# A seven-product MLP's way down: sums and weight differences moved to VectorE, results taken out of PSUM before the residual is added

## The chip, the cores and the metric

The kernel runs on one core of a Trainium2 chip. Its time is the device time of the whole program in microseconds (us). Before the change it is 2821.14 us, the median of three runs (2816.69 to 2826.64). One more execution was recorded by the hardware profiler; every row below is from it.

Engines are named as in the profile: PE multiplies matrices (PEld is its weight load), DVE is VectorE, ACT is ScalarE, POOL is GpSimd, and SP issues the DMAs. PSUM is the memory into which PE writes its products; SBUF is the working memory.

## What is computed

Two transformer blocks with cross attention follow one another, on 16 sequences of 256 tokens with 512 channels. The case is about the MLP at the end of the first block:

```python
x = x + out
h = layer_norm(x, n2_w, n2_b)
h = jax.nn.gelu(h @ fc1_w + fc1_b, approximate=False) @ fc2_w + fc2_b
return x + h
```

fc1_w is 512 x 2048 and fc2_w is 2048 x 512. The second block takes the result. It also needs a mask that tells which of its rows are zero throughout: `mask0 = 1.0 - jnp.all(x == 0, axis=2, keepdims=True)`.

## The kernel before

**Three phases.** The first block's attention comes first, then its MLP (class `Mlp0`), then the second block with two attentions and an MLP. The 4096 rows are worked on in eight groups g of 512 rows (G = 4 tiles of 128 rows).

**Seven products.** The MLP's matrix products are done two by two blocks at a time, in the manner of Strassen and Winograd: seven block products in place of eight, for which some operands are first combined with one another. For the activations there are four such combinations ("sums", made by `differences`, lines 786 to 793 of the profile), for the weights four as well (`weigh`, lines 839 to 842). Afterwards the seven results are combined into the four blocks of the output.

**Two parts for precision.** Every operand is held as a high part and a low part: ACT casts the value to the high part (line 141, `x_t` in the profile, or `w_h`), and an engine subtracts that from the value to have the low part (line 142, `c_t` or `w_l`). Each block product is then three matmuls per piece: high by high, high by low, low by high.

**Way up (`up`).** fc1 and GELU; the hidden rows of each group and quarter are stored to HBM (`hid`), 1 MB each.

**Way down (`down`, from line 1167).** 32 steps n: for each group g four quarters q of the hidden rows. A step multiplies seven operands with fc2's weights, 84 matmuls of 256 columns, in the order of products 1, 6, 2, 7, 5, 4, 3. The seven results of a group stay in seven PSUM banks over its four steps; each of them has a pool tag (`mm`, `sc`, `pt`) with as many banks as there are results of that tag, so the next group takes a bank again when the result in it has been read. While step n runs, the operands of step n + 1 are made: `sums_down(n + 1)` makes the four sums, and after each product `write` makes the high and the low part of the operand that the product has just released. There is one copy of the operands, so an operand is rewritten between its product in step n and the same product in step n + 1.

In `differences` the first, third and fourth sum are made by `pool = nc.gpsimd` and the second by `own`, which is `nc.vector` here.

**The end of a group (`end`, line 1036).** In the step with q = 3 the results are combined after each product. ACT copies the result of product 1 out of PSUM (line 1046), DVE adds the others to it or straight into the residual rows `x` out of PSUM (lines 1048 to 1063), and POOL adds the two partial results that are in SBUF into `x` (lines 1049, 1050, 1055, 1056). Then the four tiles of `x` are stored (line 1065), ACT sums their absolute values (line 1068, `junk`) and DVE turns these into the mask (line 1071).

**The residual rows.** `residual(g)` (line 1027) loads four tiles of 128 x 512 into the one buffer with tag `x1`, in the step q = 1 (q = 2 for the first group); `offset` (line 1032) adds fc2's bias to them on POOL in the step q = 3. The load can start when the rows of the group before have been stored out of that buffer.

**Order.** PE's instructions run in the order in which the program has them. For the other engines a scheduler decides the order from a simulated timeline when the kernel is built, so an instruction may stand earlier or later in its queue than the program text suggests. On each engine they then run in that fixed order. All DMAs are issued by SP.

**Weights.** `weigh(way, m)` makes the combinations of weight block m: way 1 is fc1, way 2 fc2. The first two blocks of fc1 are made early, during attention; the other six at the start of the way up, the eight of fc2 during the last group of the way up and the first two steps of the way down.

Of the kernel before, what the change touches and what calls it, by code (L numbers as in the profile page):

```python
# [10 lines left out]
F32 = mybir.dt.float32  # L11
# [3 lines left out]
AF = mybir.ActivationFunctionType  # L15
ALU = mybir.AluOpType
# [4 lines left out]
P = 128  # L21
# [7 lines left out]
G = NB * NT  # L29
N = G * P  # L30
NG = B // NB
# [10 lines left out]
def kernel(ctx: ExitStack, tc: tile.TileContext, a, out):  # L42
# [7 lines left out]
    nc = tc.nc  # L50
# [22 lines left out]
    for t, at in ((0, 0), (1, P)):  # L73
        w = (t + 1) * P
        nc.gpsimd.affine_select(
            out=tri[:, at : at + w],
            in_=tri[:, at : at + w],
# [9 lines left out]
    for i in range(NB):  # L87
        own = hmask[:, i, i * HPC : (i + 1) * HPC]
        nc.gpsimd.memset(own, 1.0)
        for base, step in ((0, 1), (D - 1, -1)):  # L90
            nc.gpsimd.affine_select(
                out=own,
                in_=own,
# [8 lines left out]
    xd = [[dram.tile([N, C], F32, name=f"xd{i}_{g}") for g in range(NG)] for i in range(4)]  # L102
# [645 lines left out]
    class Mlp0:  # L748
# [13 lines left out]
        W = 2 * P  # L762
# [20 lines left out]
                self.open_group(m)  # L783


        def differences(self, a21, a22, a11, a12, out, own):

            s1, s2, s3, s4 = out
            pool = nc.gpsimd
            pool.tensor_tensor(out=s1, in0=a21, in1=a22, op=ALU.add)  # L790
            own.tensor_tensor(out=s2, in0=s1, in1=a11, op=ALU.subtract)  # L791
            pool.tensor_tensor(out=s3, in0=a11, in1=a21, op=ALU.subtract)
            pool.tensor_tensor(out=s4, in0=a12, in1=s2, op=ALU.subtract)
# [19 lines left out]
        def weigh(self, way, m, early=False):  # L813


            view = self.raw.pop(m)
            if way == 1:
                b = [[view[:, 2 * k : 2 * k + 2, ts(n, P)] for n in range(2)] for k in range(2)]
                b2 = view[:, 2:4, :].rearrange("p k (n c) -> p n k c", n=2)
            else:  # L820
                b = [[view[:, k, ts(n, 2 * P)] for n in range(2)] for k in range(2)]
                b2 = view[:, 1, :].rearrange("p (n c) -> p n c", n=2)
            self.w[m] = tuple(
                self.wp[m][1].tile([P, 7, 2 * P], F32R, tag=f"w{x}", name=f"w{m}_{x}")
                for x in "hl"
            )
            pool = self.tmp if not early and m % 2 and (way == 1 or m == 1) else self.pool
            diff = pool.tile([P, 4, 2 * P], F32, tag="diff", name="diff")

            def like(x):  # L830
                if way == 2:
                    return x
                if len(x.shape) == 2:
                    return x.rearrange("p (k c) -> p k c", k=2)
                return x.rearrange("p n (k c) -> p n k c", k=2)

            t1, t2, t3, t4 = (like(diff[:, i, :]) for i in range(4))
            pool = nc.gpsimd
            pool.tensor_tensor(out=t1, in0=b[0][1], in1=b[0][0], op=ALU.subtract)
            pool.tensor_tensor(out=t2, in0=b[1][1], in1=t1, op=ALU.subtract)  # L840
            pool.tensor_tensor(out=t3, in0=b[1][1], in1=b[0][1], op=ALU.subtract)
            pool.tensor_tensor(out=t4, in0=b[1][0], in1=t2, op=ALU.subtract)
            h, l = self.w[m]
            for x, at in ((b[0][0], 0), (b2, slice(1, 3))):
                split_lazy(x, like(h[:, at]), like(l[:, at]), nc.gpsimd if early else nc.vector)
            split_lazy(diff, h[:, 3:], l[:, 3:], nc.gpsimd if early else nc.vector)
# [137 lines left out]
        def sums_down(self, n):  # L984
            h = self.h.pop(n)
            b = [[h[:, :, k, ts(t, self.W)] for k in range(2)] for t in range(2)]
            if n == 0:

                s = [self.up_pool.tile([P, C], F32, tag="xn", name="sums") for _ in range(2)]
                two = self.tmp.tile([P, 4, 2 * P], F32, tag="diff", name="sums")  # L990
                two = two.rearrange("p (i m) n -> p i m n", m=2)
                s = [x.rearrange("p (m n) -> p m n", m=2) for x in s] + [two[:, i] for i in range(2)]
            else:
                s = self.px.tile([P, 4, 2, self.W], F32, tag="x2", name="sums")
                s = [s[:, i] for i in range(4)]
            self.differences(b[1][0], b[1][1], b[0][0], b[0][1], s, nc.vector)
            self.a = [b[0][0], b[0][1], b[1][1]] + s

        TAGS = {1: "mm", 6: "mm", 2: "mm", 7: "sc", 5: "sc", 4: "pt", 3: "pt"}
# [33 lines left out]
                    out=x[:, t, :], in0=x[:, t, :], in1=self.b_fc2, op=ALU.add  # L1033
                )

        def end(self, g, i, x):

            add, W = nc.vector.tensor_tensor, self.W
            p = self.banks

            def block(t, c):
                return x[:, 2 * t : 2 * t + 2, ts(c, W)]

            if i == 6:
                p1 = self.flat("p1")
                nc.scalar.copy(p1, p[g, 1])
                u2 = self.u2 = self.flat("u2")
                add(u2, p1, p[g, 6], ALU.add)
                nc.gpsimd.tensor_tensor(out=block(0, 0), in0=block(0, 0), in1=p1, op=ALU.add)
                nc.gpsimd.tensor_tensor(out=block(0, 1), in0=block(0, 1), in1=u2, op=ALU.add)  # L1050
            elif i == 2:
                add(block(0, 0), block(0, 0), p[g, 2], ALU.add)
            elif i == 7:
                add(self.u2, self.u2, p[g, 7], ALU.add)
                nc.gpsimd.tensor_tensor(out=block(1, 1), in0=block(1, 1), in1=self.u2, op=ALU.add)
                nc.gpsimd.tensor_tensor(out=block(1, 0), in0=block(1, 0), in1=self.u2, op=ALU.add)
            elif i == 5:
                add(block(0, 1), block(0, 1), p[g, 5], ALU.add)
                add(block(1, 1), block(1, 1), p[g, 5], ALU.add)
            elif i == 4:  # L1060
                add(block(1, 0), block(1, 0), p[g, 4], ALU.add)
            elif i == 3:
                add(block(0, 1), block(0, 1), p[g, 3], ALU.add)
                for t in range(G):
                    nc.sync.dma_start(out=xd[1][g][ts(t, P), :], in_=x[:, t, :])
                for t in range(G):
                    junk = self.flat("junk").rearrange("p m n -> p (m n)")
                    nc.scalar.activation(
                        junk, x[:, t, :], AF.Abs, accum_out=m0[:, g, t : t + 1]
                    )  # L1070
                nc.vector.tensor_scalar(m0[:, g, :], m0[:, g, :], 0.0, None, ALU.not_equal)

        def begin(self):

# [92 lines left out]
        def down(self, early, after_up):  # L1167
            last = NG * self.NS - 1
            left, load = ExitStack(), None
            xs = {}  # L1170
            self.hidden(1)
            for n in range(last + 1):
                g, q = divmod(n, self.NS)
                if n == last - 1:

                    for m in (2, 3):
                        self.wp[m][0].close()
                    load = early()
                    pool = sbuf(left, "late2", 1)
                    load(lambda: pool.tile([P, C], F32, tag="wst", name="wst", bufs=2))  # L1180

                    late = [pool.tile([P, N], F32R, name=f"late{i}") for i in range(6)]
                    late += [self.slots[7][1]]
                if q == (1 if g else 2):
                    xs[g] = self.residual(g)
                elif q == 3:
                    self.offset(xs[g])
                if n + 1 <= last:
                    self.sums_down(n + 1)
                    self.next = self.slots  # L1190
                    if n + 1 == last:
                        self.next = [(x, s[1]) for x, s in zip(late, self.slots)]
                if n + 2 <= last:
                    self.hidden(n + 2)
                for i in (1, 6, 2, 7, 5, 4, 3):
                    if n or i not in (1, 6):
                        self.product_down(n, i)
                    if n < last:
                        self.write(self.OPS[i][0])
                    if q == self.NS - 1:  # L1200
                        self.end(g, i, xs[g])
                    if n == last and i in (1, 2, 5, 4, 3):
                        after_up((1, 2, 5, 4, 3).index(i))
                self.at = self.next
                if n < 2:
                    self.weigh(2, self.NM - 2 + n)
            left.close()
            for m in range(4, self.NM):
                self.wp[m][0].close()
            self.tmp_stack.close()  # L1210
            for m in (1, 0):
                self.wp[m][0].close()
            self.stack.close()
# [380 lines left out]
```

## Time and profile before

| what | before |
|---|---|
| median of three runs | 2821.14 us |
| the profiled execution, its time | 2812.6 us |
| its span, first to last instruction | 2810.9 us |
| PE busy, share of the span | 95% |
| DVE | 73% |
| ACT | 65% |
| POOL | 31% |
| mean granted TensorE clock | 0.986 |
| way down: first to last matmul | 1071.2 to 1457.3 us |

The shares are means over three phases that differ. Rows of groups have: line, engine, operation, output <- inputs, shapes and count, then busy us and mean ns, then the idle time of the engine just before them and what ended it. Rows of waits have: the waiting engine, tile and line, what it waited for, then us in total, times, and the longest. Rows of a chain have: start, us, and what ran. A line number belongs to the kernel before; the helper lines 141 and 142 serve all of the MLP's operands.

### The profile page before, as it was taken

How to read it: one execution, taken by the hardware profiler on the slowest of the kernel's cores; microseconds unless marked ns; L12 is line 12 of the kernel's file. 1: busy time of each engine (PE TensorE's matmuls, PEld its weight loads, DVE VectorE, ACT ScalarE, POOL GpSimd, SP SyncE). 2: the span in 40 equal slices, each digit the busy share in tenths (PEclk: the TensorE clock that was granted, in tenths of full speed). 3: DMA queues.
4: the chain of work that ended last, by engine and by line, in shares of the span. 5: the costliest groups of instructions: out<-in, count | busy, mean ns of one | idle time of the engine just before them, and what ended most of it. 6: DMA issues, size and time to landing. Idle time of an engine off the chain costs nothing.

```text
span 2810.9 us, 56659 instructions
## 1 busy us (share of the span) xinstructions
PE 2676.1 (95%) x18970; PEld 2259.4 (80%) x18970; DVE 2045.4 (73%) x5763; ACT 1823.0 (65%) x5292; POOL 862.1 (31%) x874
## 2 busy tenths in 40 slices
PE   6999999998899999999989999999999999999998
PEld 5777777776799999889887787777777777777787
DVE  7666666657756559888876777777777777777887
ACT  4877777778555555343446787787777777777532
POOL 6222211204601127666661111113322122213333
PEclk9999999999999999999999999999999999999999
DMA  6565555644323334434356665657665555556221
GB/s 230 169 193 175 174 176 171 195 158 143 127 110 135 121 144 171 150 121 150 121 190 213 196 189 182 192 183 222 205 199 172 187 185 186 188 166 183 97 93 58
DMA packets 287810, 465.41 MB, mean 166 GB/s; under 512 B 36257, under 2 KB 188321, under 8 KB 279329
## 3 DMA queue, kind: packets, MB, share of 16 engines
q1 hardware_dynamic: 287520, 461.78, 51.0%
q8 instruction: 153, 2.51, 0.4%
q14 instruction: 137, 1.11, 0.1%
HBM read 284.97 MB, written 176.69 MB: 164 GB/s over the span
## 4 chain that ended last, share of the span: by engine, by line
PE 67%; DVE 15%; DMA 7%; issue 4%; ACT 3%; POOL 3%; SPq 1%; POOLq 0%; DVEq 0%; ACTq 0%
PE ps_p L258 17%; PE ps_v L258 14%; PE ps_pt L449 8%; PE down L1015 5%; PE ps_s L408 5%; PE ps_z L468 5%; PE up_sc L902 3%; DVE c_t L142 3%; PE up_pt L902 2%; PE up_mm L902 2%; PE ps_t L277 2%; DVE st L238 1%; DMA xd<-x 1%; ACT e L433 1%; DVE e L423 1%
## 5 line engine op out<-in xcount | busy, mean ns | idle before, releaser
L433 ACT ACTIVATE e<-e,mn 128x256 f32<-128x256 f32 (+1 forms) x1024 | 487.4, 480 | 66.3 <-DVE mn L423 63.9
L455 ACT COPY pt<-ps_pt 128x512 f32<-128x512 f32 (+1 forms) x696 | 378.2, 546 | 177.5 <-PE ps_pt L449 165.5
L449 PE MATMUL ps_pt<-ident,e 128*128 128x128 f32 x2816 | 437.0, 274 | 21.8 <-DVE lbias L1255 10.0
L449 PEld LDWEIGHTS ps_pt<-ident,e 128*128 128x128 f32 x2816 | 336.3, 141 | 62.9 <-ACT pt L455 7.6
L408 PE MATMUL ps_s<-stack 97*128 97x256 f32 (+1 forms) x1536 | 331.9, 298 | 15.0 <-ACT e L433 7.1
L408 PEld LDWEIGHTS ps_s<-stack 97*128 97x128 f32 (+1 forms) x1536 | 269.5, 190 | 74.5 <-ACT e L433 14.3
L1322 POOL TENSOR_TENSOR x<-x,zz 128x256 f32<-128x256 f32 x128 | 95.5, 746 | 727.9 <-DVE zz L1315 670.2
L1015 PE MATMUL down<-w_h,c_t 128*128 128x256 f32 x900 | 264.5, 295 | 21.5 <-DVE c_t L142 21.5
L433 ACT ACTIVATE e<-ps_s,mn 128x256 f32<-128x256 f32 x512 | 241.0, 483 | 53.9 <-DVE mn L419 43.9
L1015 PE MATMUL down<-w_h,x_t 128*128 128x256 f32 x868 | 254.8, 293 | 11.0 <-ACT x_t L141 8.8
L1015 PE MATMUL down<-w_l,x_t 128*128 128x256 f32 x868 | 253.3, 292 | 0.0
L423 DVE CUSTOM_DVE_ANT_0 e<-mb,ps_s 128x256 f32<-128x256 bf16 x512 | 192.6, 415 | 76.8 <-PE ps_s L408 74.8
L242 POOL TENSOR_TENSOR rstd<-rstd,nhalf 128x1 f32<-128x1 f32 x192 | 140.6, 738 | 316.6 <-DVE rstd L241 314.4
L258 PE MATMUL ps_p<-x_t,q_h 128*128 128x512 f32 x640 | 215.2, 417 | 4.4 <-DVE qk L128 2.3
L419 DVE TENSOR_REDUCE mn<-ps_s 128x2 f32<-128x512 f32 x256 | 175.0, 684 | 48.9 <-PE ps_s L408 46.6
L468 PE MATMUL ps_z<-pt,v 128*32 128x256 f32 (+1 forms) x3072 | 200.1, 369 | 4.3 <-ACT pt L455 2.1
L1015 PEld LDWEIGHTS down<-w_h,c_t 128*128 128x128 f32 x900 | 180.8, 201 | 25.0 <-DVE c_t L142 25.0
L423 DVE CUSTOM_DVE_ANT_0 e<-tri,ps_s 128x128 f32<-128x128 f32 (+1 forms) x512 | 160.1, 346 | 53.5 <-PE ps_s L408 51.4
L433 ACT ACTIVATION_READ_ACCUMULATOR e<-e,mn 128x1 f32 x1024 | 197.4, 193 | 0.0
L1015 PEld LDWEIGHTS down<-w_h,x_t 128*128 128x128 f32 x868 | 175.2, 202 | 12.5 <-ACT x_t L141 10.0
L141 ACT CAST x_t<-sums 128x512 fp32r<-128x512 f32 x156 | 92.6, 619 | 138.0 <-DVE sums L791 89.6
L1015 PEld LDWEIGHTS down<-w_l,x_t 128*128 128x128 f32 x868 | 175.0, 202 | 0.0
(245 smaller groups left out, 7463.6 us busy)
## 6 DMA issues: line engine op xcount, KB each, us to landing
stack<-d SPq DMA_DIRECT2D x1152, 128.0 KB
d<-qk SPq DMA_DIRECT2D x192, 512.0 KB
hid<-ho SPq DMA_DIRECT2D x32, 1024.0 KB
raw<-hid SPq DMA_DIRECT2D x32, 1024.0 KB
x<-xd SPq DMA_DIRECT2D x128, 256.0 KB
xd<-x SPq DMA_DIRECT2D x96, 256.0 KB
xin<-in_x_dram SPq DMA_DIRECT2D x32, 256.0 KB
xin<-in_ctx_dram SPq DMA_DIRECT2D x32, 256.0 KB
```

The costliest lines, as they stand in the source:

```text
L242: nc.gpsimd.tensor_tensor(out=rstd[:, 1:2], in0=rstd[:, 0:1], in1=nhalf, op=ALU.pow)
L258: nc.tensor.matmul(ps, w[p], x[q], start=(k == 0 and i == 0), stop=(k == kc - 1 and i == 2))
L408: nc.tensor.matmul(ps[:, t, :], u.st[: self.rows, 0, j, ts(t, P)], u.st[: self.rows, 1, j, :], start=True, stop=True,)
L419: nc.vector.tensor_reduce(mn, ps, AX.X, ALU.min)
L423: nc.vector.tensor_tensor_reduce(out=e[:, at], in0=bias[t], in1=ps[:, t, : job.width[t]], scale=-SC, scalar=BIG, op0=ALU.add, op1=ALU.min, ...
L433: nc.scalar.activation(e[:, at], ps[:, t, :] if bias is None else e[:, at], AF.Exp, bias=mn[:, t : t + 1], scale=-1.0, accum_out=u.rs[:, t ...
L449: nc.tensor.transpose(pp[:, ts(x, P)], e[:, at : at + P], ident)
L455: nc.scalar.copy(pt[:, :n], pp[:, :n])
L468: nc.tensor.matmul(z[ts(j, D), w[0] * P :], job.v[u.i * NT + mc][:, u.c * P + j * D : u.c * P + (j + 1) * D], u.pt[j][:, x0 * P : (x0 + le ...
L902: nc.tensor.matmul(ps[:, mm, :], w[p][:, k, :], x[q][:, k, :], start=(first and mm == k == j == 0), stop=(k == 1 and j == 2), skip_group_c ...
L1015: nc.tensor.matmul(ps[:, t, :], x[p][:, mm, ts(t, P)], w[r][:, bo, :], start=(q == mm == t == j == 0), stop=(q == self.NS - 1 and mm == 1 ...
L1322: nc.gpsimd.tensor_tensor(out=xv, in0=xv, in1=zz, op=ALU.add)
```

## The change

Four things are changed; the matmuls and their order are the same.

1. `differences` has a parameter for the engine of three of its sums. `sums_down` passes `nc.vector`, so all four sums of the way down are made on DVE. The way up's sums stay on POOL.
2. `weigh` uses DVE for its four differences where the weight block isn't one of the first two of fc1 (`early`).
3. `end` no longer touches the residual rows. It combines the results into four SBUF tiles: `p1`, `u2`, `u3` (pool tag `u`, three buffers) and `c22`.
4. A new `finish` adds these four to the residual rows, on DVE, then stores the rows and has ACT sum the absolute values. It stands in the program after product 2 of the next group's first step; `tests` (the mask) and the load of the next residual rows stand at q = 2 of the next group.

```diff
-        def differences(self, a21, a22, a11, a12, out, own):
+        def differences(self, a21, a22, a11, a12, out, own, pool=nc.gpsimd):
...
-            pool = nc.gpsimd
+            pool = nc.gpsimd if early else nc.vector
             pool.tensor_tensor(out=t1, in0=b[0][1], in1=b[0][0], op=ALU.subtract)
...
-            self.differences(b[1][0], b[1][1], b[0][0], b[0][1], s, nc.vector)
+            self.differences(b[1][0], b[1][1], b[0][0], b[0][1], s, nc.vector, nc.vector)
...
-        def end(self, g, i, x):
+        def end(self, g, i):
+            add, p = nc.vector.tensor_tensor, self.banks
             if i == 6:
-                p1 = self.flat("p1")
+                p1, u2 = self.flat("p1"), self.flat("u2")
                 nc.scalar.copy(p1, p[g, 1])
-                u2 = self.u2 = self.flat("u2")
                 add(u2, p1, p[g, 6], ALU.add)
-                nc.gpsimd.tensor_tensor(out=block(0, 0), in0=block(0, 0), in1=p1, op=ALU.add)
-                nc.gpsimd.tensor_tensor(out=block(0, 1), in0=block(0, 1), in1=u2, op=ALU.add)
+                self.c = [p1, u2]
             elif i == 2:
-                add(block(0, 0), block(0, 0), p[g, 2], ALU.add)
+                add(self.c[0], self.c[0], p[g, 2], ALU.add)
             elif i == 7:
-                add(self.u2, self.u2, p[g, 7], ALU.add)
-                nc.gpsimd.tensor_tensor(out=block(1, 1), in0=block(1, 1), in1=self.u2, op=ALU.add)
-                nc.gpsimd.tensor_tensor(out=block(1, 0), in0=block(1, 0), in1=self.u2, op=ALU.add)
+                u3 = self.flat("u3")
+                add(u3, self.c[1], p[g, 7], ALU.add)
+                self.c.append(u3)
             elif i == 5:
-                add(block(0, 1), block(0, 1), p[g, 5], ALU.add)
-                add(block(1, 1), block(1, 1), p[g, 5], ALU.add)
+                c22 = self.tmp.tile([P, 4, 2 * P], F32, tag="diff", name="c22")[:, :2, :]
+                add(self.c[1], self.c[1], p[g, 5], ALU.add)
+                add(c22, self.c[2], p[g, 5], ALU.add)
+                self.c.append(c22)
...
+        def finish(self, g, x):
+            for k, c in enumerate(self.c):
+                at = x[:, 2 * (k // 2) : 2 * (k // 2) + 2, ts(k % 2, self.W)]
+                nc.vector.tensor_tensor(at, at, c, ALU.add)
+                if k % 2:
+                    for t in (k - 1, k):
+                        nc.sync.dma_start(out=xd[1][g][ts(t, P), :], in_=x[:, t, :])
+            for t in range(G):
+                junk = self.flat("junk").rearrange("p m n -> p (m n)")
+                nc.scalar.activation(junk, x[:, t, :], AF.Abs, accum_out=m0[:, g, t : t + 1])
+
+        def tests(self, g):
+            nc.vector.tensor_scalar(m0[:, g, :], m0[:, g, :], 0.0, None, ALU.not_equal)
...
-                if q == (1 if g else 2):
+                if q == 2:
                     xs[g] = self.residual(g)
+                    if g:
+                        self.tests(g - 1)
...
-                        self.end(g, i, xs[g])
+                        self.end(g, i)
+                    if q == 0 and g and i == 2:
+                        self.finish(g - 1, xs.pop(g - 1))
...
+            self.finish(NG - 1, xs.pop(NG - 1))
+            self.tests(NG - 1)
```

More of the change, by code (lines that the diff above doesn't have):

```diff
@@ L837, in weigh @@
             t1, t2, t3, t4 = (like(diff[:, i, :]) for i in range(4))
-            pool = nc.gpsimd
+            pool = nc.gpsimd if early else nc.vector
             pool.tensor_tensor(out=t1, in0=b[0][1], in1=b[0][0], op=ALU.subtract)
@@ L1034, in offset @@
                 )
-        def end(self, g, i, x):
[L1038 to L1042, printed above, removed]
+        def end(self, g, i):
+            add, p = nc.vector.tensor_tensor, self.banks
             if i == 6:
-                p1 = self.flat("p1")
+                p1, u2 = self.flat("p1"), self.flat("u2")
                 nc.scalar.copy(p1, p[g, 1])
-                u2 = self.u2 = self.flat("u2")
@@ L1060, in end @@
+                add(self.c[1], self.c[1], p[g, 5], ALU.add)
+                add(c22, self.c[2], p[g, 5], ALU.add)
+                self.c.append(c22)
             elif i == 4:
-                add(block(1, 0), block(1, 0), p[g, 4], ALU.add)
+                add(self.c[2], self.c[2], p[g, 4], ALU.add)
             elif i == 3:
-                add(block(0, 1), block(0, 1), p[g, 3], ALU.add)
-                for t in range(G):
-                    nc.sync.dma_start(out=xd[1][g][ts(t, P), :], in_=x[:, t, :])
@@ L1066, in end @@
[L1066 to L1071, printed above, removed]
+                add(self.c[1], self.c[1], p[g, 3], ALU.add)
+        def finish(self, g, x):
[8 more added lines that the diff above has]
+                nc.scalar.activation(junk, x[:, t, :], AF.Abs, accum_out=m0[:, g, t : t + 1])
```

## The prediction

> **What bounds the kernel now.** I read the page first for the engine shares: PE is busy 95% of the span, so what can be won is where PE has gaps. The table by stretches finds them. The seven-product way down of the first MLP (its matmuls run from 1071.2 to 1457.3 us) has PE gaps; the way up before it is nearly dense. Columns: stretch, its length, then busy time and instruction count of PE, PEld, DVE, ACT and POOL, then clock, DMA share and GB/s. Each stretch is about one batch group of the way down (four steps):
>
> ```profile
> 1164.00:1211.00 47.00, 44.60 (x357) 44.19 (x357) 39.32 (x43) 20.50 (x40) 30.65 (x21) 0.96 0.40 136
> 1211.00:1258.00 47.00, 42.56 (x332) 41.95 (x332) 38.47 (x40) 18.26 (x37) 29.84 (x21) 0.93 0.40 135
> ```
>
> DVE (VectorE) 38 of 47 us and POOL (GpSimd) 30 of 47: neither full, both waiting on one another. The waits of 1071 to 1458 us say so:
>
> ```profile
> ACT x_t L141 <- DVE sums L791: 89.6, 27, 7.7
> ...
> POOL sums L790 <- DVE c_t L142: 59.7, 23, 4.2
> DVE sums L791 <- POOL sums L790: 49.0, 16, 6.5
> ...
> PEld down L1015 <- DVE c_t L142: 25.0, 17, 2.5
> ```
>
> The operand sums of a step go POOL, DVE, POOL; then ACT casts and DVE makes the low part (c_t), and PE waits for that. The groups of the same stretch give the durations:
>
> ```profile
> L142 DVE TENSOR_TENSOR c_t<-sums,x_t 128x512 fp32r<-128x512 f32 x123 | 132.5, 1102 | 5.9 <-ACT x_t L141 5.7
> ...
> L793 POOL TENSOR_TENSOR sums<-raw,sums 128x512 f32<-128x512 f32 x31 | 51.1, 1649 | 10.0 <-DVE sums L791 5.6 <-DVE m L1071 4.4
> L791 DVE TENSOR_TENSOR sums<-sums,raw 128x512 f32<-128x512 f32 x31 | 49.6, 1600 | 49.0 <-POOL sums L790 49.0
> L1032 POOL TENSOR_TENSOR x<-x,b_fc 128x512 f32<-128x512 f32 x32 | 48.4, 1534 | 37.1 <-DMA x<-xd 32.9 <-ACT x_t L141 4.2
> ...
> L1059 DVE TENSOR_TENSOR x<-x,down 128x512 f32<-128x512 f32 x8 | 5.4, 676 | 0.1
> ```
>
> The reader should compare the first and last line: the same size on the same engine, 1102 ns where both inputs lie in SBUF and 676 ns where one is PSUM. The chain of waits shows the other half:
>
> ```profile
> 1223.36 0.68 DVE x L1059
> 1226.23 7.60 DMA xd<-x
> 1233.91 2.49 DMA x<-xd
> 1237.12 0.70 issue
> 1237.81 1.30 POOL x L1032
> 1239.11 1.25 POOL sums L790
> 1240.42 1.65 issue
> 1242.07 0.85 DVE c_t L142
> 1243.75 1.76 DVE c_t L142
> 1245.56 15.11 PE down L1015 x105
> ```
>
> Once a group, the finished residual is stored, the next one is loaded into the same buffer, the bias is added to it on POOL, and the sums of an unrelated step stand behind that add in POOL's queue. PE resumes at 1245.56.
>
> **What the Trainium skill says.** "SBUF — State Buffer", section "Who interferes with whom": a VectorE instruction with two SBUF inputs contends with a GpSimd instruction that reads SBUF, and one with at most one SBUF input does not. The trace agrees: 1102 against 676 ns above. "GPSIMD Engine Reference", section "Engine selection": a two-input elementwise operation is about twice as slow there. The trace agrees: L790 takes 1296 ns (its median) beside 680 for a quiet DVE one. "PSUM — Partial Sum Buffer", section "Engine vs sequencer instructions": these engines' queues are strictly first in, first out; the chain above shows it, and it is what can go wrong after the change.
>
> **The floor.** In a stretch without gaps PE starts a 256-wide matmul every 0.120 us (timeline: 1179.77, 1179.89, 1180.01). A group has 336 of them, 40.3 us; all 32 steps have 2688, 322.6 us. Inside the stage lie also two products of the way up (24 matmuls, 2.9 us) and three sets of transposes, about 1.1. Floor 326.6; the stage takes 386.1. So 59.5 us are PE gaps: about 9 in the first 20 us, 2.8 before the transposes at 1450.16 (a wait for a load), the rest about 6 in each of eight groups. From one group to the next the loads of the chain lie 46.5 us apart (1140.96 to 1419.78 in six groups), 6.2 above 40.3.
>
> **Operand sums to DVE (POOL three of four, before).** DVE gains 3 instructions a step. Back to back on DVE, quiet 128x512 adds start 0.60 us apart (1187.23, 1187.83, 1188.43). Per group DVE then has 16 sums, 28 low parts, 7 adds out of PSUM and 4 adds into the residual: 55 x 0.60 = 33.0, plus 0.16 for the test of m0. POOL keeps only four bias adds, 4 x 1.3 to 1.7 = 5.2 to 6.8 us. What contention costs: before, a group had 39 such DVE instructions, 39 x 0.60 = 23.4 us, but was busy 38.5 beside 30 us of POOL, so 0.5 us for each us of POOL. After: about 3 us. DVE needs 36 of 40.3 us: under PE, but close. The handover between POOL and DVE (49.0 and 59.7 us of waits) goes entirely.
>
> **Results leave PSUM first.** An end has 7 adds either way; the four POOL adds a group (1.3 to 1.75 us each) become four DVE adds, already counted. The adds out of PSUM no longer wait for POOL, so banks are free no later.
>
> **The residual a step later.** The order of the changed kernel's instructions puts its first two adds within the last step of the group and the last two three places into the next step, so the stores go out about as before. The load (L1027) moves to the step with q = 2 and still waits for the stores' 7.6 us in SP's queue; one load of hidden rows is queued behind its first quarter, and the other three quarters behind that. Counted from the start of the step q = 0: stores issued at about 6.5, landed by 14.5, then 2 MB; at the 4.8 us that 1 MB takes in the chain (raw<-hid at 1077.90), the hidden rows land by 21 to 24. They are needed on DVE from 21.5 and their first product starts at 30. Covered, with some 4 us left. If this cover fails, everything behind that first sum in DVE's queue waits. The bias adds now fall at about 22 to 30, on the light steps, with nothing behind them in POOL's queue.
>
> **Where DVE's peak falls.** The last step of a group has 11 + 7 instructions and one or two residual adds, 20 x 0.60 = 12 us in a step of 10.1; the next has 14, and among them the test of m0 waits for four ACT sums (0.62 + 0.19 each). Walking through the order with a cast of 0.62 before each low part, the tightest operand (third difference, in the step after the end) is ready about 0.5 us before its product; others have 3 us or more. So I leave 0.8 us of gaps a group, 6.4 in all; bounds 0 and 3 a group.
>
> **fc2's and fc1's weight differences to DVE.** 14 sets of four 128x256 subtractions, 56 x 0.41 (the like-sized DVE low part at 1056.71) = 23 us of DVE work in place of POOL's, each 0.73 to 1.2. On the way up three sets of two (721 to 754 us) meet PE waits of 5.1 us; the first differences finish earlier (DVE free at 719.7, rows there at 721.6) but the low parts of the raw weights are queued behind them. I take 0; bounds -2 to +3. At the start of the way down, the set for the sixth weight block now ends about 1080.5 where POOL ended at 1077.9, so the next hidden rows start 2.7 us later, while the sums after them are faster: PE resumes about 1091.6 where it did at 1090.98. I take 0; bounds -3 to +3.
>
> **The end of the stage.** The gap of 2.8 before the transposes came from DVE being late with the last reads of the buffer to be loaded. It should be 1 or less. The second block's instructions keep their order but for single places, so what is won stays won.
>
> **Sum.** 59.5 of gaps less 9 at the start, 1 at the end and 6.4 in the groups, less 1 of everything small: 42 to 47 us; with the start's lost clock recovered I take 46. The profiled execution took 2812.6 us (span 2810.9); 2812.6 - 46 = 2766.6. The median of the runs is 2821.1, 8.5 above; against that 2775.
>
> **Rivals.**
> (a) DVE becomes the bound: waiting adds cost 0.68 rather than 0.60, 55 x 0.68 = 37.4, plus contention 3 and waits at the head of its queue of 3 to 4: 44 us a group. The win is then 2.5 x 8 = 20 us, and with the bounds of the starts 2795 to 2803. For it: the peak of 12 us in a step of 10.1. Against: operands have six products (8.6 us) between release and use.
> (b) Everything fits: no gap in the groups and half the start's gone: 6.4 + 5 more, 2764. For it: the middle steps have 11 instructions, 6.6 us in 10.1. Against: the weight differences at the start.
> (c) Slower: the hidden rows behind the residual load in SP's queue come late and stop DVE, whose whole queue waits. The place is the load after the stores, in seven groups. To eat 46 us it must cost 6.6 us a group beyond the 4 us of cover, so rows later than 34 us after the start of q = 0; at 10 us late, 7 x 10 = 70, minus 46, gives 2845. For it: SP issues in order and DVE now waits at its head. Against: before, the same load stood behind all four quarters and ACT waited for it only 1.2 us.
>
> **Numbers.** Forecast 2775, chance 0.66, own range 2765 to 2787; (a) 0.22; (b) 0.08; (c) 0.04. Range 2761 to 2801, which takes in (b) and the larger half of (a). About 0.3% (8 us) separates a change from none here. Faster 0.94, same 0.02, slower 0.04.
>
> **What would show it.** Right: POOL busy under 8 us a group; DVE's c_t at 680 to 750 ns mean; PE's period 40.3 to 41.5 a group; no store or load of the residual in the chain. Wrong: PE waiting for c_t or x_t in the step after each end; a wait of DVE sums on the load of hidden rows; DVE busy over 39 us a group.

## The result, and the profile after

The changed kernel takes 2782.08 us (median of four runs, 2781.28 to 2783.09) beside 2819.0 us for the kernel before on the same chip (four runs; 2821.14 us was the median of the first three): ratio 0.9871, 95% interval 0.9855 to 0.9888, so 37 us less. A second comparison gave 0.9876 (0.9861 to 0.9891). The forecast was 2775 with a range of 2761 to 2801. The direction, the main mechanism and its size were right; two places at the two ends of the stage, which it priced at nothing, cost 10 us together in one trace of the changed kernel and 7 in another.

The engine shares come first again, from the page of the changed kernel:

```profile
PE 2665.7 (96%) x18970; PEld 2247.6 (81%) x18970; DVE 2057.1 (74%) x5947; ACT 1827.1 (66%) x5292; POOL 624.5 (22%) x690
```

POOL has lost 184 instructions and 238 us; DVE has the 184 more and is busy only 12 us longer. The table by stretches, one batch group each (columns as in the forecast):

```profile
1140.40:1181.30 40.90, 40.68 (x337) 40.44 (x337) 38.36 (x57) 19.74 (x38) 6.65 (x4) 1.00 0.44 156
1181.30:1222.20 40.90, 40.68 (x337) 40.44 (x337) 38.49 (x57) 19.74 (x38) 6.79 (x4) 1.00 0.43 155
```

A group takes 40.90 us in place of 46.5, with 4 POOL instructions in place of 21, and the granted clock is 1.00 where it was 0.93 to 0.96. DVE's 38.4 us for 57 instructions are 0.67 us each; in a dense row they start 0.60 us apart, which makes 34.2 us, so the column overstates what DVE needs. The groups of instructions of the way down (1068 to 1424 us):

```profile
L142 DVE TENSOR_TENSOR c_t<-sums,x_t 128x512 fp32r<-128x512 f32 x124 | 104.8, 869 | 7.5 <-ACT x_t L141 7.5
...
L142 DVE TENSOR_TENSOR c_t<-raw,x_t 128x512 fp32r<-128x512 f32 x92 | 67.3, 732 | 9.4 <-ACT x_t L141 8.9
L1031 POOL TENSOR_TENSOR x<-x,b_fc 128x512 f32<-128x512 f32 x32 | 53.4, 1688 | 281.6 <-DMA x<-xd 151.5 <-DVE c_t L142 95.9 <-DVE sums L791 34.2
...
L790 DVE TENSOR_TENSOR sums<-sums,raw 128x512 f32<-128x512 f32 x31 | 23.3, 752 | 0.0
```

The second sum took 1600 ns and waited 49.0 us for POOL before; it takes 752 and waits for nothing. The low parts fell from 1102 (and 1098 for those from `raw`) to a mean of 797, (104.8 + 67.3) / 216. They are not at 680 because some of those that meet a bias add on POOL still take 1.78 us; the ones with no POOL add beside them take 0.68. POOL itself waits for the residual's load, 151.5 us in all, and nobody waits for POOL. The waits of the same stretch:

```profile
ACT x_t L141 <- DVE sums L790: 16.9, 15, 3.1
...
PE down L1014 <- DVE c_t L142: 5.3, 11, 1.6
PE down L1014 <- ACT x_t L141: 4.5, 1, 4.5
...
DVE sums L789 <- DMA raw<-hid: 1.1, 1, 1.1
```

ACT's 89.6 us of waits for the sums are 16.9. DVE waits for hidden rows once and ACT once, both in the first steps, so the hidden rows behind the residual's load cost nothing. PE waits for a low part 11 times: three times in the first steps, once in the last, and once after each of seven group ends. The chain of waits tells what these seven are:

```profile
1176.89 0.87 ACT junk L1069 x3
...
1178.04 0.80 ACT junk L1069 x3
1178.84 0.51 ACT x_t L141
1179.35 0.62 ACT junk L1069 x2
1179.98 0.52 ACT x_t L141
1180.50 0.03 issue
1180.52 0.70 DVE c_t L142
1181.22 0.04 issue
1181.27 35.92 PE down L1014 x297
```

Neither the residual's store nor its load is in it any more. Once a group ACT's sums of absolute values (`junk`) stand ahead of the cast of an operand, its low part follows, and PE resumes. That is the 0.6 us between 40.9 and the floor of 40.3; `no_m0` below tests it.

**Where the 37 us came from.** The two kernels run the same matmuls in nearly the same order, so the start of one matmul in one trace can be set against its start in the other. The difference at a few points, and its steps, in us (minus is earlier than before):

```
from .. to, in the time of before      step
start of the program .. 1075 us        +1.7
1075 .. 1110, start of the way down    +4.1
1110 .. 1436, the eight groups        -43.3
1436 .. 1453, the transposes           -1.7
1453 .. 1501, start of second block    +6.2
1501 .. end                            +2.4
end                                   -30.6
```

The profiled execution of before was 6 us under its own median, so its trace shows a saving of 30.5 us where the medians show 37. The first and last rows are spread between executions: the changed kernel profiled twice gave +1.7 and +0.2 in the first, +2.4 and +14.9 in the last, where the granted clock varies. The four rows between are the change, and they repeat to 2.4 us or better. So the experiments below are read in these four rows first, and by the ratio second.

The row of the groups can be taken apart. At 0.12 us a matmul, the kernel before has 47.3 us too much there. Of these, 32.1 lie in 25 gaps. Another 13.6 lie in 149 matmuls that start 0.213 us apart, because the granted clock is 0.50 there: eight stretches of 3.4 or 6.8 us, about one a group, each at the group's gaps (from 1243.8 to 1250.7 us, for example). The changed kernel has 4.0 us too much in all and no such stretch in its groups, and neither have the kernels below that show no gap there. So more than a quarter of what was won came with the gaps but lay in the matmuls behind them.

### The profile page after: what moved, and what is told of

It reads as the page before. It is cut to its first block, busy times and chain, and to the rows that moved or that the text cites. A ratio compares the mean times of both kernels' runs of the same rounds, so it can differ in the third digit from the quotient of the medians.

```text
span 2780.4 us, 56655 instructions
## 1 busy us (share of the span) xinstructions
PE 2665.7 (96%) x18970; PEld 2247.6 (81%) x18970; DVE 2057.1 (74%) x5947; ACT 1827.1 (66%) x5292; POOL 624.5 (22%) x690
## 4 chain that ended last, share of the span: by engine, by line
PE 54%; DVE 10%; DMA 3%; issue 2%; ACT 2%; POOL 1%; SPq 1%; POOLq 0%; DVEq 0%; ACTq 0%
PE ps_p L258 12%; PE down L1014 9%; PE ps_v L258 9%; PE ps_pt L449 5%; PE up_sc L901 4%; PE ps_s L408 4%; PE ps_z L468 3%; PE up_pt L901 2%; PE up_mm L901 2%; DVE c_t L142 1%; PE ps_t L277 1%; DVE st L238 1%; DVE x L252 1%; PE ps_z L1320 1%; DMA stack<-d 1%
## 5 line engine op out<-in xcount | busy, mean ns | idle before, releaser
L1014 PE MATMUL down<-w_h,c_t 128*128 128x256 f32 x900 | 256.4, 286 | 5.3 <-DVE c_t L142 5.3
L1014 PE MATMUL down<-w_h,x_t 128*128 128x256 f32 x868 | 247.7, 285 | 4.5 <-ACT x_t L141 4.5
L1014 PE MATMUL down<-w_l,x_t 128*128 128x256 f32 x868 | 246.8, 284 | 0.0
L1014 PEld LDWEIGHTS down<-w_h,c_t 128*128 128x128 f32 x900 | 173.6, 193 | 7.8 <-DVE c_t L142 7.8
L1014 PEld LDWEIGHTS down<-w_h,x_t 128*128 128x128 f32 x868 | 167.9, 193 | 4.9 <-ACT x_t L141 4.7
L1014 PEld LDWEIGHTS down<-w_l,x_t 128*128 128x128 f32 x868 | 167.8, 193 | 0.0
L468 PEld LDWEIGHTS ps_z<-pt,v 128*32 128x32 f32 x3072 | 83.6, 109 | 101.4 <-issue 29.7
```

What stands on the lines that cost most here:

```text
L468: nc.tensor.matmul(z[ts(j, D), w[0] * P :], job.v[u.i * NT + mc][:, u.c * P + j * D : u.c * P + (j + 1) * D], u.pt[j][:, x0 * P : (x0 + le ...
L1014: nc.tensor.matmul(ps[:, t, :], x[p][:, mm, ts(t, P)], w[r][:, bo, :], start=(q == mm == t == j == 0), stop=(q == self.NS - 1 and mm == 1 ...
```

## The experiments

The table sets each kernel against the trace of before in the same way: "start", "groups", "tail" (the transposes) and "second" (the start of the second block) are the four rows, and "sum" is over them. The texts under each heading below say what each kernel is.

```
kernel           start  groups   tail  second   sum    ratio (95% interval)
changed           +4.1   -43.3   -1.7    +6.2  -34.7   0.9871 (0.9855 to 0.9888)
after_again       +1.7   -42.8   -2.3    +5.6  -37.8   0.9876 (0.9861 to 0.9891)
sums_only         -0.9   -47.2   +2.0    -0.7  -46.9   0.9844 (0.9826 to 0.9862)
sums_again         0.0   -47.3   +2.1    -1.7  -46.9   0.9848 (0.9835 to 0.9862)
end_only          +0.2   -21.6   +0.3    +6.1  -14.9   0.9948 (0.9933 to 0.9963)
sums_weigh        +4.4   -47.3   +2.1    +1.3  -39.5   0.9854 (0.9831 to 0.9876)
weigh_pool        -1.1   -42.8   -2.3    +5.0  -41.2   0.9857 (0.9842 to 0.9872)
pool_reads       +11.2   +18.5   -3.5    +5.9  +32.1   1.0127 (1.0112 to 1.0142)
residual_early    +4.2   -41.8   -3.4    +6.4  -34.6   0.9884 (0.9864 to 0.9904)
no_m0             +1.8   -47.3   -1.0    +1.5  -45.0   0.9848 (0.9833 to 0.9863)
last_stores       +4.4   -43.3   -0.1    +5.4  -33.6   0.9877 (0.9862 to 0.9891)
no_last_m0        +4.4   -43.3   -1.6    +1.1  -39.4   0.9872 (0.9859 to 0.9886)
```

### The sums alone, and the results and residual alone

`sums_only` is the kernel before with the first edit only:

```diff
-            self.differences(b[1][0], b[1][1], b[0][0], b[0][1], s, nc.vector)
+            self.differences(b[1][0], b[1][1], b[0][0], b[0][1], s, nc.vector, nc.vector)
```

(`differences` takes its POOL engine as an argument, as in the change.)

> The kernel before with one edit: the operand sums of the way down on VectorE. Theory A (the 6.2 us of gaps per group came from the POOL-DVE handover of the sums and from standing behind the bias adds in POOL's queue): nearly the whole group gain comes with this edit alone; PE period 41 to 42 us per group, POOL about 13 us per group, c_t under 800 ns, time 2778 to 2788 us. Rival B (the store, load and bias of the residual is what costs): period stays above 45 us and the time above 2808 us.

`end_only` is the changed kernel with this edit and that of `weigh` undone.

> The changed kernel with operand sums and fc2's differences back on GpSimd, so that only the results leaving PSUM first and the residual's later load remain. Theory A: the handover stays, so at most a third of the gain: period 45 to 46.5 us per group, time 2805 to 2822 us, ACT and DVE still waiting on POOL's sums. Rival B (the residual is what costs): period under 43 us, time under 2795 us.

The sums alone take 2770.34 us and win all of the groups, 47.2 us, 4 more than the whole change and more than I had expected of them. A group of this kernel, in the table by stretches:

```profile
1178.60:1219.00 40.40, 40.40 (x339) 40.40 (x338) 39.30 (x53) 19.99 (x37) 13.23 (x8) 1.00 0.46 155
```

PE has no gap at all, although POOL still has 13 us a group, eight adds into the residual and of the bias. The c_t mean, which I expected under 800 ns, is 900 and 916; that is DVE beside 13 us of POOL, and it is hidden.

`end_only` wins 21.6 us in the groups, half of the changed kernel's 43.3, with 2800.87 us and about 43.5 us a group. Theory A had allowed it a third at most and 2805 to 2822, the rival a period under 43 and less than 2795, so both theories mis-sized it. Its waits show what is left, the handover of the sums:

```profile
POOL sums L789 <- DVE c_t L142: 97.5, 25, 7.8
...
DVE sums L790 <- POOL sums L789: 36.6, 29, 3.8
PEld down L1014 <- DVE c_t L142: 18.9, 15, 2.5
```

The two parts cure the same gap. The sums of the next step were late because they stood behind the bias adds in POOL's queue and those waited for the residual. Moving the residual takes away a part of that; taking the sums out of POOL's queue takes away all. 47.2 and 21.6 can't be added: there were only 47.3 us to win, and together they win 43.3.

### The weight differences

`weigh_pool` is the changed kernel with `weigh` on GpSimd again; `sums_weigh` is the sums alone with `weigh` moved as well.

```diff
-            pool = nc.gpsimd if early else nc.vector
+            pool = nc.gpsimd
```

> The changed kernel with fc2's (and fc1's) weight differences back on GpSimd. Theory A: they cost 4.1 us at the start of the way down, since the raw weights are read later on DVE and hidden rows of step 1 wait for that buffer in SP's queue, and about 1.5 us in the early way up; so 2776 to 2779 us, rows of step 1 issued about 1078 and PE resuming about 1091 us in the way down. Rival: the differences on POOL contend with DVE's first sums and the start is no better: 2782 us within 2, the same first 30 us of the way down.

> The kernel before with the operand sums and the weight differences on VectorE (the first two edits; results and residual as before). Theory A: the weight differences cost some 4 us at the start of the way down here as well, the period stays 40.4 us per group and nothing is lost at the start of the second block: 2774 to 2777 us where the sums alone take 2770. Rival: their cost comes only together with the later residual; then 2770 within 2 us.

The start of the way down goes from +4.1 (+1.7 in the second trace of the changed kernel) to -1.1 when they are back on POOL (2776.02 us, with a ratio whose interval overlaps that of the changed kernel), and from -0.9 to +4.4 when they are put on DVE beside the sums alone (2779.48 us, with runs from 2771.61 to 2791.94). Theory A holds in both directions, but for the 1.5 us in the early way up, of which nothing came back. By the time alone `sums_weigh` can't be told from the sums alone, which took 2778.36 us on that chip; by the four rows it is 7.4 us behind them (-39.5 for -46.9), 5 of them at the start. What happens shows in SP's queue (SPq). The DMA issues of before (start, length of the issue, line, operation, output <- input, count):

```profile
1070.52 0.34 SPq L941 DMA_DIRECT2D hid<-ho  x1
1077.90 1.07 SPq L981 DMA_DIRECT2D raw<-hid  x2
1081.57 0.32 SPq L941 DMA_DIRECT2D hid<-ho  x1
```

and of the changed kernel:

```profile
1072.26 0.34 SPq L940 DMA_DIRECT2D hid<-ho  x1
1078.30 0.34 SPq L980 DMA_DIRECT2D raw<-hid  x1
1082.53 0.32 SPq L940 DMA_DIRECT2D hid<-ho  x1
1082.94 13.99 SPq L980 DMA_DIRECT2D raw<-hid  x2
```

The hidden rows of step 1 (issued at 1077.90 and 1082.94) go into the buffer of the sixth set of raw weights, so they wait for the last of its four differences. Before, that is on POOL and ends at 1077.87:

```profile
1077.13 0.74 POOL L842 TENSOR_TENSOR diff<-raw,diff 128x256 f32<-128x256 f32 x1
```

In the changed kernel it stands among DVE's other work and ends at 1082.69:

```profile
1082.28 0.41 DVE L841 TENSOR_TENSOR diff<-raw,diff 128x256 f32<-128x256 f32 x1
```

The load now also stands behind the last store of the way up in SP's queue, but that place costs it at most the 0.25 us from 1082.69 to 1082.94. The store's 1 MB then moves while the load does. The load's end is in the chain of the changed kernel:

```profile
1082.94 6.99 DMA raw<-hid
...
1090.02 0.69 DVE sums L789
...
1097.15 0.04 issue
1097.19 2.93 PE down L1014 x12
```

It takes 6.99 us where the same load took 4.79 before, and PE resumes at 1097.19 where it did at 1090.98. This trace is 1.7 us late before the stage begins. Less that, the load goes out 3.3 us later, takes 2.2 us longer, and PE resumes 4.5 us later (4.3 in the second trace of the changed kernel). What is left of it at 1110 us, +4.1 or +1.7, also depends on the clock: it is granted at 0.50 for 6.8 us here before, for 10.2 us in the first trace after and for 6.8 in the second. In `weigh_pool` both loads go out together ahead of the store again:

```profile
1082.12 0.99 SPq L980 DMA_DIRECT2D raw<-hid  x2
1085.79 0.32 SPq L940 DMA_DIRECT2D hid<-ho  x1
```

I had expected these loads at about 1078 and PE at 1091; they are 4 us later, because this execution was already 4.2 us later before the stage began.

### Is it the handover, or the reading of SBUF by GpSimd?

`pool_reads` gives POOL its three adds a step back, as adds whose result nobody reads:

```diff
+            for k in range(3 if 0 < n < 30 else 0):
+                waste = self.waste.rearrange("p (m n) -> p m n", m=2)
+                nc.gpsimd.tensor_tensor(out=waste, in0=b[0][0], in1=b[0][1], op=ALU.add)
...
```

(The lines that are left out allocate the tile `waste`.)

> The changed kernel with three additional GpSimd adds of 128x512 per step of the way down (27 steps), which read the hidden rows and write a tile that nobody reads: POOL is as busy as before the change, but nobody waits for it. The output is unchanged. Theory A with contention at 0.5 us of DVE per us of POOL: DVE needs 36 + 10 = 46 us per group, so the period goes to about 46 us and most of the gain is lost: 2810 to 2825 us, c_t at 1000 ns or more. Rival C (only the handover cost time, contention is hidden under PE): period below 42.5 us and 2780 to 2792 us.

It takes 2851.36 us: not only is the whole gain gone, it is 1.3% slower than before. One group:

```profile
1202.30:1252.30 50.00, 43.67 (x336) 42.71 (x336) 49.83 (x56) 18.71 (x37) 30.41 (x17) 0.94 0.35 128
```

DVE is full, 49.83 of 50.00 us with 56 instructions, and nobody waits for POOL's result. At 0.60 us from start to start, 57 instructions take 34.2 us. Over five stretches of 50.00 us POOL was busy 29.4 us each, so each us of POOL costs DVE (50.0 - 34.2) / 29.4 = 0.54 us. I had taken 0.5, and multiplied it by 20 us of POOL. But POOL's bias adds are there too, and the adds themselves take 1955 ns, so it is 29 us and the period 50 in place of 46. Rival C falls: with POOL's reads back, contention makes DVE the bound though no one waits for POOL. So taking away the handover is not enough by itself; moving the sums took away both, and no run leaves the handover and takes away the contention alone. The contention agrees with what the Trainium skill says in "SBUF — State Buffer", section "Who interferes with whom", that DVE instructions with two inputs in SBUF and GpSimd's reads of SBUF contend; the 0.54 is this trace's.

### The load of the residual a step later

`residual_early` issues it with q = 1 again, and nothing else.

```diff
-                if q == 2:
+                if q == (1 if g else 2):
                     xs[g] = self.residual(g)
+                if q == 2:
                     if g:
                         self.tests(g - 1)
```

> The changed kernel with the load of the next residual issued in the step q = 1 as before, instead of q = 2. Theory A (nobody waits for the residual any more, since the bias adds have nothing behind them): the same within 2 us, period 40.9 us per group. Rival (the later load is what keeps hidden rows from being stuck behind it): the hidden rows come late and DVE waits, 2 to 5 us per group, so 14 us or more slower than the changed kernel.

Groups and tail together are -45.2 us against -45.0 of the changed kernel: nothing, and the 2 to 5 us a group of the rival do not come. Its median of 2789.26 us is higher, but its trace has that difference before and after the stage (+6.0 before 1075, +9.1 after 1501), not in it, and the intervals of the ratios overlap. So where the load stands is worth nothing in either direction once the sums have left POOL.

### ScalarE's sums for the mask

`no_m0` leaves out the sums of absolute values and the test, and sets m0 to one.

> The changed kernel without the four sums per group on ScalarE for the test of m0 and without the test itself; m0 is set to one instead, so this part of the computation is left out. Theory A (0.5 to 0.6 us of PE gap per group, because the cast of the third difference stands behind these sums on ScalarE): the period goes from 40.9 to 40.3 us per group and the stage ends 4 us earlier. Rival (DVE is what is late after an end, with 18 to 20 instructions in a step): period stays at 40.8 or more.

```profile
1180.30:1220.60 40.30, 40.30 (x338) 40.30 (x337) 38.05 (x56) 17.18 (x29) 6.91 (x4) 1.00 0.44 158
```

The period is 40.3 and the groups win 47.3 us, 4 more than the changed kernel. DVE's residual adds are all still there, so DVE's peak after an end is not what makes PE wait. The run takes sums and test away together and doesn't part them; the chain of the changed kernel names ACT's queue. It also did what I had not asked of it: the second block no longer starts late (+1.5 for +6.2). That led to the next one.

### The start of the second block

`last_stores` issues the stores of the last group's residual from POOL's queue:

```diff
-                        nc.sync.dma_start(out=xd[1][g][ts(t, P), :], in_=x[:, t, :])
+                        (nc.gpsimd if g == NG - 1 else nc.sync).dma_start(
+                            out=xd[1][g][ts(t, P), :], in_=x[:, t, :]
+                        )
```

> The changed kernel with the four stores of the last group's residual issued from GpSimd's queue instead of SyncE's; nothing else differs. Theory D (the second block starts 6 us late because its weight loads and score-operand spills stand behind these stores, which the last finish on DVE makes 1.6 us later): the 5 to 6 us come back, so about 0.2% less than the changed kernel, 2773 to 2777 us on a chip where that takes 2780, and PE's shift against before no longer drops between 1450 and 1500 us. Rival E (the loads wait for the memory that the finish on DVE still holds, or for DVE itself, which is late with the second block's first low parts): within 2 us of the changed kernel, with the same 6 us lost.

Theory D falls: +5.4 is left of +6.2, and 2784.19 us with a ratio of 0.9877 is the changed kernel's. The order of SP's queue tells more. A spill stores score operands to HBM (`d<-qk`), and a read-back fetches them again (`stack<-d`). In the kernels that lose 5 to 6 us here (changed in both traces, `end_only`, `weigh_pool`, `pool_reads`, `last_stores`, `residual_early`), the fourth spill stands behind most of the read-back of the second; in those that lose 1.5 us at most (before, the sums alone in both traces, `sums_weigh`, `no_m0`), ahead of it. The third spill has moved too, ahead of the first read-back. Before:

```profile
1471.13 1.34 SPq L389 DMA_DIRECT2D stack<-d  x2
1472.51 0.49 SPq L393 DMA_DIRECT2D stack<-d  x1
1473.10 0.39 SPq L378 DMA_DIRECT2D d<-qk  x1
...
1476.14 0.33 SPq L378 DMA_DIRECT2D d<-qk  x1
1477.33 0.92 SPq L389 DMA_DIRECT2D stack<-d  x2
```

The changed kernel:

```profile
1435.87 0.97 SPq L389 DMA_DIRECT2D stack<-d  x2
1437.17 0.30 SPq L393 DMA_DIRECT2D stack<-d  x1
...
1439.88 1.51 SPq L389 DMA_DIRECT2D stack<-d  x2
1442.02 0.34 SPq L378 DMA_DIRECT2D d<-qk  x1
```

From the transposes (1450.2 and 1411.0) the fourth spill goes out 26 us later before and 31 us later after. The next operand is cast into the buffer that this spill reads, and PE waits for the cast:

```profile
ACT qk L132 <- DMA d<-qk: 9.9, 3, 7.5
PEld ps_e L1253 <- ACT qk L132: 6.4, 1, 6.4
PE ps_e L1253 <- ACT qk L132: 6.0, 1, 6.0
```

`no_last_m0` is the changed kernel without the four ACT sums and the test of the last group alone (its m0 is set to one), which makes the builder's scheduler put the spill ahead again.

```diff
-            for t in range(G):
+            for t in range(G if g < NG - 1 else 0):
...
```

> The changed kernel with the four ScalarE sums and the test of m0 left out for the last group alone (its m0 is set to one, so this part of the computation is left out). By the program order of SyncE this puts the fourth spill of score operands back ahead of the second read-back of spills, as it was before the change. Theory F (the 6 us at the start of the second block are this place in SyncE's queue: the fourth spill waits there for an earlier spill to land and come back): 4 to 6 us come back between 1440 and 1480 us of the changed kernel, the period of the groups stays 40.9 us; time about 2775 where the changed kernel takes 2780. Rival E (the last finish on DVE is what is late): 0 to 1.5 us come back.

Its SP queue:

```profile
1443.01 0.33 SPq L378 DMA_DIRECT2D d<-qk  x1
1444.19 0.83 SPq L389 DMA_DIRECT2D stack<-d  x2
```

5.1 us come back (+1.1 for +6.2), with the groups unchanged at -43.3. The time did not show it: 2785.87 us beside 2787.23 of the changed kernel on that chip, because this execution lost more outside the stage (+8.2 after 1501). The trace decides for theory F over rival E. One reservation: the run also spares ACT some 3 us at that moment, so a part of the 5 us may be that. No run moved the place in the queue alone, and a part of the loss is again the clock: the changed kernel is granted 0.50 for 6.8 us from 1448.3 us, `no_last_m0` is not.

### The sums alone beside the changed kernel

> The kernel with the sums alone once more, beside the changed kernel on one chip: 10 us less than the changed kernel if its three other parts cost 4 us (start), 4 us (ScalarE sums in the groups) and 5 us (second block) against it less what they win; within 3 us of it if the first comparison came from the chip.

> The changed kernel itself, for the comparison on one chip: ratio to before 0.987.

On one chip the sums alone take 2778.36 us (2776.32 to 2779.72) and the changed kernel 2787.23 us (2783.52 to 2789.96), 8.9 us or 0.3% apart. The intervals of their ratios to before just touch (0.9835 to 0.9862, and 0.9861 to 0.9891); the first comparison had 0.9844 against 0.9871. In the traces the four rows sum to -46.9 both times, against -34.7 and -37.8. So the first of the four edits is worth more than all four together.

## Why the prediction was right, and where it missed

- **Floor and period.** 40.3 us a group and gaps of 6.2, of which 0.8 were to stay: measured 40.9, so 0.6 stay. The eight groups won 43.3 us.
- **Operand sums to DVE.** "DVE needs 36 of 40.3 us: under PE, but close": right, PE stays the bound. Contention was taken at 0.5 us per us of POOL and measured at 0.54; `pool_reads` shows that it is no small term. The closeness is partly luck: the 0.5 set busy time against the 0.60 us spacing of a dense row, in a stretch that was not dense. With the 0.68 us of a single instruction it is (38.5 - 39 x 0.68) / 30 = 0.40.
- **"1102 against 676 ns".** The pair did not show contention: seven of the eight adds of line 1059 have no POOL add beside them. The trace does show it elsewhere: all eight adds of line 1058, also out of PSUM, run beside a POOL add and take 676 ns on average, while the low parts of before take 679 ns alone and 1418 on average beside POOL.
- **Results leave PSUM first, the residual a step later.** The cover of 4 us held. But the forecast gave these parts no price against the sums alone: it did not ask whether the first edit already removed the wait that they are for. It did. In the groups they cost 4 us (-43.3 for -47.2) by putting ACT's sums ahead of a cast.
- **The tightest operand.** Its size was right, 0.6 us for 0.8. PE waits for the operand of product 6, which is the second sum (line 790, third in DVE's queue; "third difference" fits only if it is counted there). I had put it to DVE's test waiting for the four ACT sums; the chain shows ACT's own queue, the sums ahead of that operand's cast. So the number came out nearer than its reason.
- **Weight differences, "I take 0; bounds -3 to +3".** For the start of the way down this is the first mis-sized term: +4.1 in the first profile, +1.7 in the second, some 3 to 5 by the two experiments. The delay of the hidden rows was foreseen with 2.7 us and was 3.3. That their load would take 2.2 us longer beside a store of 1 MB was not foreseen.
- **The end of the stage.** Gap before the transposes "1 or less": 1.8 us.
- **"The second block's instructions keep their order but for single places, so what is won stays won."** This step failed. Two spills changed places in SP's queue, and the start of the second block lost 5 to 6 us.
- **Sum.** Forecast 46, measured 37. The terms as written make 42; the other 4 were for the clock at the start, which did not come back (0.50 for 10.2 or 6.8 us, 6.8 before). The stage itself fell from 386 us to 345 in one trace and 343 in the other, 41 and 43 us, so within it the 42 held. Without the two misses (4.1 and 6.2) the four rows would be -45.0.
- **Rivals.** (a) fell: 38.4 us busy and a period of 40.9, not 44. (c) fell: DVE waited for hidden rows once, 1.1 us. Nor did "everything fits" (b) come about, because of ACT. Of the signs named, POOL under 8 us (6.5 to 7.0), the period and the missing residual in the chain came true; the c_t mean of 680 to 750 did not (797), which cost nothing. One sign of being wrong came true as well, PE waiting for a low part in the step after an end, at 0.6 us a group.

## What to carry to other kernels

When a change has several parts, ask of each what is still late once the others are in: here the first part removed the wait, and the rest only moved work next to other deadlines. Moving work off an engine also takes away what that engine's reads cost its neighbour (0.54 us per us here), so count both. And when a scheduler writes the queues, compare the order of the DMA queue also after the stage that was edited, instruction by instruction; a place that looks like a detail decides when a spill goes out. Look at the clock in the trace, too: a gap can cost more than its length.

## What was not expected of the hardware

- Three unread adds a step on GpSimd made VectorE the bound: 56 instructions took 49.8 us in place of about 34, 0.54 us per us of GpSimd, and GpSimd's own adds took 1955 ns.
- The means of 0.93 to 0.96 in the groups before are a clock of 1.00 and, about once a group, of 0.50 for 3.4 or 6.8 us, though no gap there is longer than 2.6 us. Matmuls start 0.213 us apart in these stretches and 0.120 outside them. They cost 13.6 us of the 47.3 in the groups. `pool_reads` has them too (a mean of 0.94); the groups of the changed kernel, with gaps of 0.4 us, have none.
- A load of 1 MB took 4.79 us beside another load that was issued 0.39 us after it, and 6.99 us (6.88 in the second trace) where it was issued 0.41 us after a store of 1 MB.
- Two executions of the changed kernel differed by 7.8 us at the end although the slower one was 4.7 us ahead at 1500 us: it fell behind after that, at a granted clock of 0.97 against 0.98 (1800 to 2000 us) and 0.99 against 1.00 (2000 to 2600), with three stretches of 0.50 after 2000 us that the other does not have before its end. Effects of 5 us had to be read from the stage, not from the total.
